# Local transformer: one head pair a step, or two pairs a step with keys kept in place

## The chip, the cores and the metric

The kernel runs on one core of one Trainium2 chip, in one launch. The metric is the device time in microseconds (us) of the whole launch; lower is better. Engines are named as in the profile: PE (matrix multiplies; PEld its weight loads), DVE, ACT and POOL (element-wise work; ACT also has the exponential and the GELU), SP (issues the DMAs).

## The reference, cut to what matters

The program is a stack of four blocks over `x` of 16 sequences, 256 tokens, 128 channels, in float32. Block 1 (a linear attention with an MLP), block 3 (multi-query attention) and block 4 (an MLP) are the same before and after the change. Block 2 is a local transformer of six layers, and all of the change lies there:

```python
for i in range(6):
    x = attn_layer(shift_tokens(x), Wqkv[i], q_scale[i], k_scale[i], Wo[i]) + x
    x = ffn_layer(shift_tokens(x), ...) + x
# attn_layer: 16 heads of 64 channels
q = l2norm(q) * qs;  k = l2norm(k) * ksc
q = q * cos * scale + rotate_half(q) * sin * scale
k = k * cos / scale + rotate_half(k) * sin / scale
# local_attention: windows of 32 queries see 64 keys (their own window and the one before)
sim = einsum(bq, bk2) * 8; sim = where(mask, -max, sim)
out = einsum(softmax(sim), bv2);  return out @ Wo
```

## The kernel before, in words

The 16 sequences are eight units of two (512 tokens). A unit's state `z` (128 channels on the partitions) stays in SBUF through the six layers, with 32 columns of zeros ahead of each sequence. The work of block 2 goes in steps, one for each layer, unit and pair of heads: 6 x 8 x 8 = 384 steps. The main loop is the `while` at the end of the stage (from L986); step `n` starts pair `n` and carries on older pairs, so that some ten pairs are in flight:

- `project` (pair n): two multiplies make q and k of the pair in two PSUM banks (L645). From each bank DVE makes the sine part `sent` (L646) and the cosine part (L650; `q` or `k`), and ACT the squares (`sq`, L652). Four DMAs (L656, L657) swap the halves of `sent` between partitions into `got`.
- `rotate` (pair n-1): POOL adds `got` to q and to k (L662).
- Every fourth step `norms_sum` (L670) sums the squares of four pairs on PE with the selector `sel`; `norms_inverse` makes inverse square roots (transposes L688, small POOL operations L706 to L714); one step later `norms_rows` (L722, L724) sends the keys' ones to DRAM.
- `widened` (pair n-6): two DMAs (L733) bring a key factor to all rows, `kn`.
- `scaled` (pair n-7): POOL multiplies k by kn into one of two padded buffers, `kf` (L744). The seven buffers of the unpadded k come free only with this operation.
- `masked`, `softmax` (pair n-8): a bf16 multiply writes the mask into two PSUM banks (`sim`, L770; one bank for each head, half of it used), and 32 small multiplies add the scores (L785; each in two passes, so 64 instructions), for which PE works as eight tiles of 64x32. Then the maxima (L797), `nb` (L801, maximum times factor) and eight exponentials with their sums (L803, ACT).
- `divided` (L815, L817): reciprocal on DVE, product on POOL. `flipped` (pair n-9): four transposes (L826) and a copy into `prT` (L832 or L834).
- `attended`, a generator for each unit that moves one place a step: `windows` transposes the state (L755); the weighted sums `mm<-prT,xw` (L864, 64x128 tiles) are made for 64 tokens a step; eight multiplies a step (L847, `y`) merge heads. The values and the output weight are multiplied ahead, in `merge_vo`. After it `ffn` (L902 to L955), also one place a step.

PE is thus used whole (128x128) for projections, merging, transposes and the feed-forward part, and in tiles for L864, L670 and L785. PSUM has four banks for everything called `mm`, three for `sim`, one for `y`.

The order on each engine is made when the program is built, by a planner: the source order is a priority, and an instruction whose inputs, by the planner's own cost tables, are not ready is passed by a later one. On the chip each engine then follows the fixed order and waits where it must. In the trace this is seen where twelve passes of L785 stand ahead of L864, although the source has all of L864 first.

Of the kernel before, what the change touches and what calls it, by code (L numbers as in the profile page):

```python
# [10 lines left out]
F32 = mybir.dt.float32  # L11
# [8 lines left out]
NU = B // 2  # L20
# [24 lines left out]
def adaln_kernel(  # L45
# [504 lines left out]
    with ExitStack() as es:  # L550
# [25 lines left out]
        kfs = [persistent(f"kf{j}", (128, 2, PAD + L)) for j in range(2)]  # L576
# [58 lines left out]
        def project(i, u, wqk):  # L635
# [3 lines left out]
            rows, squares = [], []  # L639
            sent, got = atile("sent", (128, 2, 512)), atile("got", (128, 2, 512))  # L640
            for j, name in enumerate(("q", "k")):
# [7 lines left out]
                r = atile(name, (128, 512), 8 - j)  # L649
                nc.vector.scalar_tensor_tensor(two(r), two(pp), scale, tab[0], ALU.mult, ALU.mult)  # L650
                sq = work("sq")
                nc.scalar.activation(sq, pp, AF.Square)  # L652
                rows.append(r)
# [4 lines left out]
            return rows, squares, got  # L658

        def rotate(rows, got):  # L660
            for j in range(2):
                nc.gpsimd.tensor_tensor(rows[j], rows[j], got[:, j, :], ALU.add)  # L662
# [19 lines left out]
        def norms_inverse(n2):  # L682
# [34 lines left out]
            return rk, rq.rearrange("p (a b) t -> p a b t", b=2)  # L717
# [11 lines left out]
        def widened(j, home):  # L729

            kn = atile("kn", (128, 512))
            for par in range(2):
                nc.sync.dma_start(  # L733
                    kn[64 * par : 64 * par + 64, :],
                    home[2 * j + par : 2 * j + par + 1]
                    .rearrange("e t p -> e (t p)")
                    .to_broadcast([64, 512]),
                )
            return kn

        def scaled(m, k, kn):

            kf = kfs[m % 2]
            nc.gpsimd.tensor_tensor(kf[:, :, PAD:], two(k), two(kn), ALU.mult)  # L744
            return kf
# [20 lines left out]
        def masked():  # L766
            sims = []
            for par in range(2):
                sim = pss.tile([128, 512], F32, tag="sim", name="sim")[:, 0:256]
                nc.tensor.matmul(  # L770
                    sim, ident16, maskb, start=True, stop=False, skip_group_check=True
                )
                sims.append(sim)
            return sims

        def softmax(sims, q, kf, rn):

            q = two(q)
            for st in range(4):
                s = st // 2  # L780
                for c in range(4):
                    t0 = (st % 2) * 128 + 32 * c
                    for par in range(2):
                        r = slice(64 * par, 64 * par + 64)
                        nc.tensor.matmul(  # L785
                            sims[par][32 * c : 32 * c + 32, st * 64 : (st + 1) * 64],
                            q[r, s, t0 : t0 + 32],
                            kf[r, s, t0 : t0 + 64],
                            start=False,
# [3 lines left out]
            pr = atile("pr", (128, 4, 2, 64))  # L793
            ssum = small("ssum", (128, 4, 2))
            for par in range(2):
                mx = small("mx", (128, 4))
                nc.vector.tensor_reduce(  # L797
                    mx, sims[par].rearrange("p (b k) -> p b k", b=4), AX.X, ALU.max
                )
                nb = small("nb", (128, 4))  # L800
                nc.vector.scalar_tensor_tensor(nb, mx, -1.0, rn[:, par, :], ALU.mult, ALU.mult)  # L801
                for st in range(4):
                    nc.scalar.activation(  # L803
                        pr[:, st, par, :],
                        sims[par][:, st * 64 : (st + 1) * 64],
                        AF.Exp,
                        bias=nb[:, st : st + 1],
                        scale=rn[:, par, st : st + 1],
                        accum_out=ssum[:, st, par : par + 1],
                    )  # L810
            return pr, ssum

        def divided(pr, ssum):
            rsum = small("rsum", (128, 8))
            nc.vector.reciprocal(rsum, ssum.rearrange("p t h -> p (t h)"))  # L815
            prf = pr.rearrange("p t h k -> p (t h) k")
            nc.gpsimd.tensor_tensor(  # L817
                prf, prf, rsum.unsqueeze(2).to_broadcast([128, 8, 64]), ALU.mult
            )
            return pr  # L820

        def flipped(p, pr, prT):

            pt = bank()
            for st in range(4):
                nc.tensor.transpose(  # L826
                    pt[:, st * 128 : (st + 1) * 128],
                    pr[:, st].rearrange("p h k -> p (h k)"),
                    ident,
                )  # L830
            if p % 2:
                nc.vector.tensor_copy(prT[:, p, :], pt)  # L832
            else:
                nc.scalar.copy(prT[:, p, :], pt)  # L834

        def attended(u, prT, vo):


            xw = windows(u, 0)
            yield  # L840
            py = psy.tile([128, 512], F32, tag="y", name="y")
            zxs = {}
            for k in range(10):
                if k >= 2:
# [11 lines left out]
                if k < 8:  # L856
                    if k % 2 == 0:
                        zxs[k // 2] = atile("zx", (128, 2, NP, 128))
# [555 lines left out]
```

## Time and profile before

| what | us |
|---|---|
| median of three runs (4742.04 to 4749.64) | 4749.21 |
| the profiled execution | 4745.02 |
| its span, first to last instruction | 4743.2 |
| first and last start of the projections L645 | 407.5 and 3987.2 |
| PE, DVE, ACT, POOL busy | 4280.3, 2887.7, 2922.1, 2621.8 |
| L645, L847, L864, L785 busy on PE | 772.7, 753.9, 533.1, 360.7 |
| L803 busy on ACT (exponentials, and reading their sums) | 1195.6 and 639.5 |
| L662 (q and k), L744, L817 busy on POOL | 488.4 and 489.2, 490.9, 400.7 |

The span runs from the first to the last instruction of one profiled execution; 1.8 us of that execution lie around it. PE's busy time counts pipelined multiplies as overlapping stretches, so 90% is not PE at its peak. Idle time is given with the instruction that ended it.

### The profile page before, as it was taken

What the parts mean: (1) busy time and instruction counts of PE and PEld (TensorE: products, weight loads), DVE (VectorE), ACT (ScalarE), POOL (GpSimd) and SP (SyncE); (2) the same over time, 40 slices, a digit from 0 to 9 for tenths busy, and PEclk for the clock granted to TensorE, in tenths of its full rate; (3) what the DMA queues carried; (4) which work ended last, traced back from release to release, by engine and by line L of the source; (5) the groups of instructions that cost most, each with busy time, mean ns of one, the idle gap of its engine ahead of it and who ended that gap; (6) DMA issues with size and microseconds to landing.
All of it is one profiled execution on the core that took longest, in us unless ns stands there. A gap on an engine that the chain in (4) does not pass through costs nothing.

```text
span 4743.2 us, 121371 instructions
## 1 busy us (share of the span) xinstructions
PE 4280.3 (90%) x46105; PEld 2711.0 (57%) x46105; DVE 2887.7 (61%) x6755; ACT 2922.1 (62%) x9846; POOL 2621.8 (55%) x3296
## 2 busy tenths in 40 slices
PE   6677689999999999999999999999999999799998
PEld 4443356666666666666666666666666666455454
DVE  3434456666676666766666666666666666455554
ACT  2332456666666666666666666666666666277776
POOL 3323556666666666666666666656666665044342
PEclk7678789999999999999999999999999999899999
DMA  1023234433433334444344343333433333200000
GB/s 29 5 34 93 75 77 104 98 100 93 102 98 100 98 98 100 100 97 98 95 101 100 96 102 95 98 98 96 102 95 98 94 96 82 64 1 6 5 3 7
DMA packets 193567, 371.25 MB, mean 78 GB/s; under 512 B 42537, under 2 KB 83416, under 8 KB 192984
## 3 DMA queue, kind: packets, MB, share of 16 engines
q1 hardware_dynamic: 192984, 363.50, 31.2%
q8 instruction: 364, 5.96, 0.5%
q14 instruction: 219, 1.79, 0.1%
HBM read 127.92 MB, written 8.91 MB: 29 GB/s over the span
## 4 chain that ended last, share of the span: by engine, by line
PE 37%; POOL 16%; ACT 15%; issue 13%; DVE 10%; DMA 5%; SPq 2%; POOLq 0%; DVEq 0%; ACTq 0%
ACT pr L803 7%; PE mm L864 5%; PE y L847 4%; PE mm L645 3%; PE sim L785 3%; POOL kf L744 3%; POOL q L662 3%; DMA got<-sent 3%; POOL k L662 2%; PE mm L955 2%; PE mm L670 2%; DVE mx L797 2%; PE mm L945 2%; POOL pr L817 2%; DVE sent L646 2%
## 5 line engine op out<-in xcount | busy, mean ns | idle before, releaser
L803 ACT ACTIVATE pr<-sim,nb,rq 128x64 f32<-128x64 f32 x3072 | 1195.6, 409 | 521.5 <-DVE nb L801 470.5
L645 PE MATMUL mm<-z,wqk 128*128 128x512 f32 x1536 | 772.7, 626 | 4.0 <-DMA wqk<-in_L_ffn_Wqkv_dram 3.1
L847 PEld LDWEIGHTS y<-zx,wvo 128*128 128x128 f32 x6144 | 728.6, 192 | 74.4 <-issue 72.4
L847 PE MATMUL y<-zx,wvo 128*128 128x128 f32 x6144 | 753.9, 276 | 1.2 <-ACT zx L879 1.2
L817 POOL TENSOR_TENSOR pr<-pr,rsum 128x512 f32<-128x512 f32 x384 | 400.7, 1043 | 500.3 <-DVE rsum L815 468.4
L803 ACT ACTIVATION_READ_ACCUMULATOR pr<-sim,nb,rq 128x1 f32 x3072 | 639.5, 208 | 0.0
L662 POOL TENSOR_TENSOR q<-q,got 128x512 f32<-128x512 f32 x384 | 488.4, 1272 | 248.1 <-DMA got<-sent 219.0
L646 DVE SCALAR_TENSOR_TENSOR sent<-mm,vec,rope 128x512 f32<-128x512 f32 x768 | 569.2, 742 | 45.5 <-PE mm L645 36.6
L864 PE MATMUL mm<-prT,xw 64*128 64x256 f32 x3072 | 533.1, 406 | 66.6 <-ACT sq L652 65.4
L652 ACT ACTIVATE sq<-mm 128x512 f32<-128x512 f32 x768 | 437.3, 620 | 237.2 <-DVE k L650 205.8
L744 POOL TENSOR_TENSOR kf<-k,kn 128x512 f32<-128x512 f32 x384 | 490.9, 1279 | 123.5 <-PE sim L785 55.8
L877 DVE COPY zx<-mm 128x512 f32<-128x512 f32 x384 | 262.8, 684 | 433.1 <-PE mm L864 429.7
L662 POOL TENSOR_TENSOR k<-k,got 128x512 f32<-128x512 f32 x384 | 489.2, 1274 | 0.0
L864 PEld LDWEIGHTS mm<-prT,xw 64*128 64x128 f32 x3072 | 324.4, 186 | 249.5 <-issue 103.8
L650 DVE SCALAR_TENSOR_TENSOR k<-mm,vec,rope 128x512 f32<-128x512 f32 x384 | 285.0, 742 | 261.7 <-POOL kf L744 259.4
L797 DVE TENSOR_REDUCE mx<-sim 128x4 f32<-128x256 f32 x768 | 289.8, 419 | 232.9 <-PE sim L785 224.9
L785 PEld LDWEIGHTS sim<-kf,q 64*32 64x32 f32 x24576 | 280.3, 107 | 263.5 <-issue 177.5
L879 ACT COPY zx<-mm 128x512 f32<-128x512 f32 x384 | 227.6, 593 | 300.2 <-PE mm L864 300.0
L785 PE MATMUL sim<-kf,q 64*32 64x64 f32 x24576 | 360.7, 227 | 46.8 <-POOL kf L744 46.5
L645 PEld LDWEIGHTS mm<-z,wqk 128*128 128x128 f32 x1536 | 267.8, 195 | 224.9 <-issue 153.2
L1174 POOL TENSOR_TENSOR pr<-pr,rsum 128x256 f32<-128x256 f32 (+1 forms) x256 | 206.4, 828 | 318.8 <-DVE rsum L1172 294.4
L706 POOL TENSOR_TENSOR na<-nx,ny 128x64 f32<-128x64 f32 x288 | 92.4, 321 | 405.2 <-DVE ny L699 390.1
(237 smaller groups left out, 6973.7 us busy)
## 6 DMA issues: line engine op xcount, KB each, us to landing
got<-sent SPq DMA_DIRECT2D x1536, 128.0 KB
kn<-rkh SPq DMA_DIRECT2D x768, 128.0 KB
xw<-xw SPq DMA_DIRECT2D x96, 256.0 KB
wqk<-in_L_ffn_Wqkv_dram SPq DMA_DIRECT2D x48, 128.0 KB
bhome<-brow SPq DMA_DIRECT2D x1, 3072.0 KB
wv<-in_L_ffn_Wqkv_dram SPq DMA_DIRECT2D x12, 256.0 KB
wo<-in_L_ffn_Wo_dram SPq DMA_DIRECT2D x12, 256.0 KB
xt<-in_x_dram SPq DMA_DIRECT2D x8, 256.0 KB
```

What stands on the lines that cost most here:

```text
L645: nc.tensor.matmul(pp, wqk[:, j, :], xs, start=True, stop=True)
L646: nc.vector.scalar_tensor_tensor(two(sent[:, j, :]), two(pp), scale, tab[1], ALU.mult, ALU.mult)
L650: nc.vector.scalar_tensor_tensor(two(r), two(pp), scale, tab[0], ALU.mult, ALU.mult)
L652: nc.scalar.activation(sq, pp, AF.Square)
L662: nc.gpsimd.tensor_tensor(rows[j], rows[j], got[:, j, :], ALU.add)
L744: nc.gpsimd.tensor_tensor(kf[:, :, PAD:], two(k), two(kn), ALU.mult)
L785: nc.tensor.matmul(sims[par][32 * c : 32 * c + 32, st * 64 : (st + 1) * 64], q[r, s, t0 : t0 + 32], kf[r, s, t0 : t0 + 64], start=False, s ...
L797: nc.vector.tensor_reduce(mx, sims[par].rearrange("p (b k) -> p b k", b=4), AX.X, ALU.max)
L803: nc.scalar.activation(pr[:, st, par, :], sims[par][:, st * 64 : (st + 1) * 64], AF.Exp, bias=nb[:, st : st + 1], scale=rn[:, par, st : st ...
L817: nc.gpsimd.tensor_tensor(prf, prf, rsum.unsqueeze(2).to_broadcast([128, 8, 64]), ALU.mult)
L847: nc.tensor.matmul(py[:, st * 128 : (st + 1) * 128], vo[:, h, :], zxs[st][:, h % 2, h // 2, :], start=(h == 0), stop=(h == 2 * NP - 1), sk ...
L864: nc.tensor.matmul(pz[par][:, j * 256 : (j + 1) * 256], xw[r, (2 * k + j) % 8, :], prT[r, :, 64 * k + 32 * j : 64 * k + 32 * j + 32], star ...
```

## The change

Steps of two pairs: 192 steps in place of 384 (`QS = NP // 2`). The parts of a step are put in a new order, written out by hand: first the whole-array work (merging, transposes of probabilities, norms' rows, feed-forward, windows, mask), then the tiled work in one stretch (weighted sums, every second step the sums of squares, the scores), then norms' transposes, feed-forward and the two projections. The softmax is split in functions; the exponentials of head 0 of both pairs are placed ahead of the first projection, those of head 1 between the projections, the division after them. Maxima, `nb`, mask and division handle two pairs in one instruction. `attended` is replaced by `weighted` and `merging`, called from the loop. The feed-forward generator is moved twice a step, and its GELUs (L941) join the piece of the gate multiplies before them (L934) (`go_on(behind)`).

Keys are written by `project` into eight padded buffers `ks`, rotated there and multiplied by `kn` there; the copies `kf` and their two buffers go. `pr` has one buffer of 1024 columns in place of two of 512. The selector and the index `e` are permuted to match. The diff, cut to its core:

```diff
-        kfs = [persistent(f"kf{j}", (128, 2, PAD + L)) for j in range(2)]
+        ks = [persistent(f"k{j}", (128, 2, PAD + L)) for j in range(8)]
...
+            q = two(atile("q", (128, 512), 8))
+            k = ks[m % 8][:, :, PAD:]
...
-                r = atile(name, (128, 512), 8 - j)
-                nc.vector.scalar_tensor_tensor(two(r), two(pp), scale, tab[0], ALU.mult, ALU.mult)
+                nc.vector.scalar_tensor_tensor(r, two(pp), scale, tab[0], ALU.mult, ALU.mult)
...
-            kf = kfs[m % 2]
-            nc.gpsimd.tensor_tensor(kf[:, :, PAD:], two(k), two(kn), ALU.mult)
+            k = ks[m % 8][:, :, PAD:]
+            nc.gpsimd.tensor_tensor(k, k, two(kn), ALU.mult)
...
+            if 0 <= n - 4 < N:
+                for x in range(2):
+                    scaled(2 * (n - 4) + x, kns.pop(2 * (n - 4) + x))
             if 0 <= n - 1 < N:
-                rotate(rows[n - 1], got.pop(n - 1))
+                for x in range(2):
+                    m = 2 * (n - 1) + x
+                    rotate(m, qs[m], got.pop(m))
...
+                merging(j, range(NP), zxs[w, j], vos[w // NU], pys[w])
+            if 0 <= n - 5 < N:
...
+                flipped(p, prs.pop(n - 5), prTs[i, u])
+            if at_w:
+                merging(j, range(NP, 2 * NP), zxs.pop((w, j)), vos[w // NU], pys[w])
...
+            if n % 2 and 3 <= n <= N + 1:
+                home = norms_rows(rk)
+            go_on(behind)
+            go_on(merges)
...
+                    xws[v, s] = windows(v % NU, s)
+            sims = masked() if 0 <= n - 4 < N else None
...
+                zxs[v, r] = weighted(r, xws[v, r // 2], prTs[v // NU, v % NU])
+            if n % 2 == 0 and 2 <= n <= N:
+                n2 = norms_sum([squares.pop(m) for m in range(2 * n - 4, 2 * n)])
+            if sims:
+                m = 2 * (n - 4)
+                rn = inverses[m // 4][:, m % 4 // 2]
+                scores(sims, m, [qs.pop(m), qs.pop(m + 1)])
+                pr = atile("pr", (128, 2, 4, 2, 64), 1)
+                ssum = small("ssum", (128, 2, 4, 2))
+                nbs = [maxima(sims[par], rn[:, par]) for par in range(2)]
+                exponentials(0, sims[0], nbs[0], rn[:, 0], pr, ssum)
+
+            if n % 2 == 0 and 2 <= n <= N:
+                rk, inverses[n // 2 - 1] = norms_inverse(n2)
+            if at_w and j == QS - 1:
+                behind.append(ffn(w % NU, w // NU, *wff))
+            go_on(behind)
             if n < N:
...
+                qs[m], squares[m], got[m] = project(i, u, m, wqk[p])
+            if sims:
+                exponentials(1, sims[1], nbs[1], rn[:, 1], pr, ssum)
+            if n < N:
+                m = 2 * n + 1
+                qs[m], squares[m], got[m] = project(i, u, m, wqk[p + 1])
+            if sims:
+                divided(pr, ssum)
+                prs[n - 4] = pr
+            if 0 <= n - 3 < N:
+                for m in (2 * (n - 3), 2 * (n - 3) + 1):
+                    kns[m] = widened(m, home)
```

New functions that it calls:

```python
def maxima(sim, rn):
    mx = small("mx", (128, 8))
    nc.vector.tensor_reduce(mx, sim.rearrange("p (b k) -> p b k", b=8), AX.X, ALU.max)
    nb = small("nb", (128, 8))
    nc.vector.scalar_tensor_tensor(nb, mx, -1.0, rn, ALU.mult, ALU.mult)
    return nb

def exponentials(par, sim, nb, rn, pr, ssum):
    for x in range(2):
        for st in range(4):
            b = 4 * x + st
            nc.scalar.activation(pr[:, x, st, par, :], sim[:, b * 64 : (b + 1) * 64], AF.Exp,
                bias=nb[:, b : b + 1], scale=rn[:, b : b + 1],
                accum_out=ssum[:, x, st, par : par + 1])

def weighted(j, xw, prT):
    zx = atile("zx", (128, 2, NP, 128))
    for k in (2 * j, 2 * j + 1):
        pz = [bank(), bank()]
        ...  # the four multiplies of L864 and the two copies of L877, L879, as before
    return zx

def merging(j, heads, zx, vo, py):
    for h in heads:
        nc.tensor.matmul(py[:, j * 128 : (j + 1) * 128], vo[:, h, :], zx[:, h % 2, h // 2, :],
            start=(h == 0), stop=(h == 2 * NP - 1), skip_group_check=True)
```

## The prediction

> **What bounds the kernel now.** The page first: its span, and PE's row.
>
> ```profile
> span 4743.2 us, 121371 instructions
> PE 4280.3 (90%) x46105; PEld 2711.0 (57%) x46105; DVE 2887.7 (61%) x6755; ACT 2922.1 (62%) x9846; POOL 2621.8 (55%) x3296
> ```
>
> PE is the engine with least room. The source view of the projections runs from 407.5 to 3987.2 us, so the 384 pairs take 3580 us: 9.32 us a pair, 18.65 for two pairs, 74.6 for a unit of eight. Only these 3580 us are touched; the other 1165 of the profiled 4745 stay. The table of stretches for them:
>
> ```profile
> 407.00:3987.00 3580.00, 3307.13 (x41019) 2156.73 (x41020) 2337.93 (x4760) 2297.85 (x8020) 2240.20 (x2842) 0.98 0.39 97
> ```
>
> PE 92%, the others 63 to 65%: no other engine becomes the bound by its sum, since none gains much work. What PE loses is read from its timeline (start, duration with overlap, instruction):
>
> ```profile
> 2213.64 1.95 PE L847 MATMUL y<-zx,wvo 128*128 128x128 f32 x16
> 2215.42 0.38 PE L770 MATMUL sim<-maskb,ident 128*128 128x256 bf16 x2
> 2215.73 1.14 PE L864 MATMUL mm<-prT,xw 64*128 64x256 f32 x8
> 2216.80 0.86 PE L785 MATMUL sim<-kf,q 64*32 64x64 f32 x64
> 2217.59 1.98 PE L645 MATMUL mm<-z,wqk 128*128 128x512 f32 x4
> ```
>
> Sixteen passes of L847 take 1.78 us from start to start, 0.111 each; so L770's two end at 2215.64 and the tiles start 0.09 late. Four pass times of 256 columns, side by side on two row tiles, would be 0.86 (the six passes of 512 of L955 just before take 2.58, 0.43 each), but L785 starts after 1.07: 0.21 lost. The last score pass runs out before L645: some 0.14 of its 0.216. Entering, changing and leaving tiles costs about 0.44 a pair.
>
> The waits of PE over the same stretch, largest first (us, times, longest):
>
> ```profile
> PE mm L670 <- ACT sq L652: 71.7, 46, 2.7
> PE mm L864 <- ACT sq L652: 65.4, 86, 1.1
> PE sim L785 <- POOL kf L744: 46.5, 15, 5.7
> PE sim L770 <- ACT pr L803: 30.6, 48, 1.2
> PE mm L945 <- ACT sq L652: 23.8, 29, 1.1
> ```
>
> Most end with a square. Behind L670's stands this, in the timeline around 2241 us:
>
> ```profile
> 2239.90 1.26 POOL L744 TENSOR_TENSOR kf<-k,kn 128x512 f32<-128x512 f32 x1
> 2241.20 0.75 DVE L650 SCALAR_TENSOR_TENSOR k<-mm,vec,rope 128x512 f32<-128x512 f32 x1 [4.05 <-POOL kf L744]
> ...
> 2241.99 0.60 ACT L652 ACTIVATE sq<-mm 128x512 f32<-128x512 f32 x1 [2.40 <-DVE k L650]
> ...
> 2242.64 3.62 PE L670 MATMUL mm<-sq,sel 128*32 128x512 f32 x16 [2.36 <-ACT sq L652]
> ```
>
> A new k needs one of seven buffers, free only after L744; DVE stands 4.05 us, the square behind it, then PE. L650 waits so 116 times, 259.4 us in all. All the waits of PE there make about 260 us, 5.4 a unit.
>
> **What the skill says.** The Trainium skill, TensorEngine Tiling (Array Packing), Key Properties: changing the tiling mode drains TensorE. The 0.09, 0.21 and 0.14 agree. TensorE: Matmul & The Clock Gate, Part 1: a PE idle for a window of about 3.4 us falls to half clock. Here 2.36 us of idleness sufficed: L670's 16 passes took 3.62 where they take 1.92 elsewhere. SBUF — State Buffer, Who interferes with whom: a DVE instruction with two SBUF inputs blocks behind a GpSimd one that reads SBUF. `nb` (L801) is one: median 152 ns, mean 334, longest 1267, about one POOL product.
>
> **The change part by part, for two pairs.**
>
> *Work.* Multiplies, transposes, exponentials, squares, copies and DMAs are as many as before. Two L797 of 419 ns become one of 512 columns for each head, at about 0.68 (L877, 512 columns from PSUM, takes 684), four `nb` become two, two reciprocals one: DVE saves under 1 us, hidden under PE. L770 has half as many instructions of double width: nothing. Key products into rows of 2x256: L744 wrote such rows at 1279 ns, against 1274 for flat L662: nothing. Six more buffers to clear: a few us once on POOL, before its first rotation; if not covered, that.
>
> *Tiles.* One stretch in place of two saves 0.44, 192 x 0.44 = 84 us if the order holds. If one whole-array instruction falls inside, 0.09 + 0.21 come back.
>
> *Keys.* The wait for L744 goes: k's buffer is free when the scores of four steps ago are done, and these stand before the projection on PE. What is late next is the square itself: those of the second projection come behind the second set of exponentials on ACT, and the sums of squares want them some 6 us of PE work later. Of the 166 us of PE's waits on squares (five lines, three of them above) I take 105 as gone, 2.2 a unit; bounds 0 and 166, plus some 20 for the slow clock.
>
> *Queues.* Rotations have a step of 18.65 us instead of 9.32 for their transfers. `got` has two buffers, both used in one step now, but their refill comes a step later, behind the rotation. SP issues eight `got` and four `kn` DMAs a step at about 0.6 us: 7.2 of 18.65. `kn` is issued at the end of a step and wanted before the scores of the next, with `scaled` first on POOL. Nothing new is late.
>
> *Softmax.* This is where the change adds a wait. From the last score to the transposes of its probabilities:
>
> - DVE: two maxima, 2 x 0.68 = 1.36, and `nb`, 0.3 to 0.7: 1.9 with ACT's start;
> - ACT: eight exponentials 0.382 apart (2219.17 to 2219.57 and on, from ACT's timeline): 3.06; two squares that stand between, 1.11; eight more, 3.06;
> - DVE reciprocal and its handing on, 0.4; POOL, 1024 columns at twice L817's 1.04: 2.1.
>
> Sum 11.6 us. Before it was about 5.5 with a step of 9.3 and the projection to cover it; `flipped` stood after the next projection. Now it stands after 8 heads of merging. In source order PE has for cover: norms' transposes 0.22, four projections' passes 2 x 1.72 = 3.44, half the feed-forward (538 us busy over six lines, 11.2 a unit, 2.8 a step) 1.4, merging 1.78: 6.8. PE would stand 4.8 us. Then transposes 0.88, merging 1.78, feed-forward 1.4, windows 0.44, mask 0.43, L864 2.0, half of L670 0.92, scores 1.44: 9.3. Step 11.6 + 9.3 = 20.9, or 2.25 more than 18.65: 192 x 2.25 = +430 us.
>
> But the planner does not hold source order. Three lines of PE's timeline:
>
> ```profile
> 2222.05 0.33 PE L785 MATMUL sim<-kf,q 64*32 64x64 f32 x12
> 2222.92 1.62 PE L864 MATMUL mm<-prT,xw 64*128 64x256 f32 x8 [0.54 <-ACT sq L652]
> 2224.46 0.76 PE L785 MATMUL sim<-kf,q 64*32 64x64 f32 x52
> ```
>
> L864 is ahead of L785 in the source; the planner, expecting it late, passed it, and on the chip it was later still by 0.54. So I expect it to pass `flipped` with the second merging, feed-forward, windows and mask, 1.78 + 1.4 + 0.44 + 0.43 = 4.05: cover 10.85 against 11.6. The transposes land at the door of the tiled stretch, PE waiting 0.7, or just inside it at 0.3 for two more changes. But they stand where the planner's tables say ready, with no slack; what the chip does later is all wait. Bounds: 0, and some 1.7 (nb blocked twice by POOL adds 2 x 1.1 to the chain, less what PE's own lateness gives). I take 0.4 a step.
>
> *Sum for a unit*: tiles -0.9 (half of 4 x 0.44), keys -2.2, softmax +1.6 (4 x 0.4): -1.5. Times 48 = -72, on 4745: 4673; the profiled run is 4 below the median of 4749, so 4677.
>
> **The rivals.**
>
> 1. *The softmax's chain reaches PE.* Same mechanism with a larger wait. It decides at (0.9 + 2.2) x 48 / 192 = 0.78 us a step at the transposes; above it the change loses. For: zero slack, chain doubled, POOL's products across `nb`. Against: the 9.5 us for which PE waited at L826 in the whole stage before. At 1.5 us: 192 x (1.5 - 0.78) = +138, 4887. With source order in full, 4749 + 430 = 5180. Chance 0.30 for the first, 0.12 for the second.
> 2. *PE's waits nearly go*: tiles whole (-84), squares (-166, and -20 of slow clock), transposes 0.3 (+58): -212, 4537. For: twice the time for every transfer and norm. Against: ACT still has the gates (three copies of 0.58, three GELUs of 0.72, two table loads of 1.28: 6.5 us in one piece, once a unit) ahead of copies that free `mm` banks. Chance 0.12.
> 3. *The change does not do what it says*: the planner strews whole-array work through the stretch (no gain from tiles) and the squares' wait goes over to the banks that they hold: within 0.2%, 4749. Chance 0.06.
>
> The forecast has 0.40.
>
> **How the numbers follow.** Faster 0.40 + 0.12, same 0.06, slower 0.42; 0.2%, 9 us, is about what three runs can tell. Likeliest: 4677, its own range 4600 to 4735 (keys from 0 to all, wait from 0 to 0.75). The range for 8 in 10: down to 4510 for the second rival with a little more, up to 4920 for waits to 1.7 us; left out are source order (0.12) and the tails.
>
> **What would show it.** Right: L785 and L864 with no L826 between, starts of L864 0.3 later half as often; no wait of L650 on POOL; L670's wait on squares under 25 us; L826's wait on POOL's `pr` under 80 us (192 x 0.4). Wrong: L826 (or whatever stands there) waiting 200 us or more; a PE clock below 0.98 in the stage; a step over 18.65 us. If `mm` banks rule, L864 or L902 will wait on ACT's copies and squares.

## The result, and the profile after

| | us |
|---|---|
| before, median of 4 runs (4742.04 to 4750.96) | 4749.43 |
| after, median of 4 runs (4961.98 to 4982.88) | 4973.42 |
| after / before, 95% interval | 1.0474 [1.0449, 1.0498] |
| the profiled execution of after, and its span | 4973.54, 4971.8 |
| first and last start of the projections (L647) after | 408.6 and 4229.5 |

The change makes the kernel 224 us slower. The whole loss lies in block 2: its projections start over 3821 us where they took 3580. A step of two pairs takes 19.9 us against 18.65.

The page of after, its span and PE's row:

```profile
span 4971.8 us, 118780 instructions
PE 4346.0 (87%) x45721; PEld 2814.7 (57%) x45721; DVE 2782.6 (56%) x5795; ACT 2929.3 (59%) x9846; POOL 2586.0 (52%) x3110
```

PE has 384 instructions fewer and is busy 66 us longer; the rest of the span, in which it is not busy, grew from 462.9 to 625.8 us. A busy time that grows with less work to do can be a sign of the clock. The table of stretches, the same columns as before (PE, PEld, DVE, ACT, POOL busy, then the granted clock as a share of full speed, the DMA share and GB/s):

```profile
407.00:4229.00 3822.00, 3379.57 (x40687) 2263.61 (x40688) 2239.14 (x3827) 2308.70 (x8036) 2203.19 (x2658) 0.92 0.36 91
```

The clock fell from 0.98 to 0.92. The two longest waits of PE over this stretch (us, times, longest):

```profile
PE mm L834 <- POOL pr L825: 331.3, 143, 5.1
PE sim L769 <- ACT pr L812: 50.1, 59, 6.9
```

The waits on squares, which made three of the five lines shown of before, are gone; one wait that was 9.5 us there is now 331: the transposes of the probabilities (`flipped`, L834) for the division on POOL (L825). DVE's wait of 259.4 us for a free k buffer is no longer among DVE's waits at all. PE's timeline shows one such wait, and what follows it:

```profile
2228.20 1.48 PE L791 MATMUL sim<-k,q 64*32 64x64 f32 x128
...
2230.97 3.60 PE L647 MATMUL mm<-z,wqk 128*128 128x512 f32 x8
2234.40 3.73 PE L873 MATMUL y<-zx,wvo 128*128 128x128 f32 x32
2237.97 0.59 PE L769 MATMUL sim<-maskb,ident 128*128 128x512 bf16 x2
2238.50 0.90 PE L791 MATMUL sim<-k,q 64*32 64x64 f32 x68
2242.25 1.51 PE L834 MATMUL mm<-ident,pr 128*128 128x128 f32 x8 [2.86 <-POOL pr L825]
...
2243.77 1.71 PE L906 MATMUL mm<-mean,fs 128*128 128x1 f32 x8
2245.41 0.42 PE L791 MATMUL sim<-k,q 64*32 64x64 f32 x4
2245.76 1.91 PE L753 MATMUL mm<-ident,z 128*64 128x128 f32 x8
```

Three things are to be seen. PE goes on from the last score of a step at 2229.62 and starts its transposes at 2242.25, 12.63 us later; PE has work for 9.77 of them. The step is typical: counted in the trace, the transposes wait in 147 of the 192 steps, and over these the mean is 12.30 us, of which 9.99 are covered. Work of the next step has been put ahead of the transposes: both halves of the merging (L873), the mask (L769), here half of the scores (L791). The feed-forward piece (L906) and the windows (L753), which do not need the division either, stand behind. And the tiled stretch that the change wanted in one piece is broken: scores (L791) stand on both sides of the transposes.

The chain itself, from scores to divided probabilities, is on the other engines' timelines. DVE's maxima start at 2229.71 (two in 1.29 us), `nb` follows at 2231.03 and 2231.58 (0.50 and 1.17 us, the second beside a POOL product). ACT runs the first eight exponentials from 2231.64, three squares from 2234.71 and the other eight from 2236.67 to 2239.7; DVE's reciprocal starts at 2239.90. The last step of it, on POOL:

```profile
2240.30 1.90 POOL L825 TENSOR_TENSOR pr<-pr,rsum 128x1024 f32<-128x1024 f32 x1 [2.09 <-DVE rsum L823]
```

POOL stood idle for 2.09 us before the division: it was the chain that was late, not POOL. Counted in the trace, it stood so before the division in 144 of the 147 steps that wait.

### The profile page after: what moved, and what is told of

It is laid out like the page before. It is cut to its first block, busy times and chain, and to the rows that moved or that the text cites. A ratio compares the mean times of both kernels' runs of the same rounds, so it can differ in the third digit from the quotient of the medians.

```text
span 4971.8 us, 118780 instructions
## 1 busy us (share of the span) xinstructions
PE 4346.0 (87%) x45721; PEld 2814.7 (57%) x45721; DVE 2782.6 (56%) x5795; ACT 2929.3 (59%) x9846; POOL 2586.0 (52%) x3110
## 4 chain that ended last, share of the span: by engine, by line
PE 42%; ACT 21%; POOL 9%; issue 9%; DVE 7%; DMA 3%; SPq 2%; POOLq 0%; DVEq 0%; ACTq 0%
ACT pr L812 13%; POOL pr L825 6%; PE mm L834 5%; PE mm L647 4%; PE mm L852 4%; PE y L873 4%; PE mm L670 4%; DMA kn<-rkh 3%; PE mm L951 3%; PE mm L930 2%; PE mm L941 2%; ACT sq L653 2%; PE sim L791 2%; PE mm L753 2%; DVE sent L648 2%
## 5 line engine op out<-in xcount | busy, mean ns | idle before, releaser
L873 PEld LDWEIGHTS y<-zx,wvo 128*128 128x128 f32 x6144 | 721.5, 192 | 99.4 <-issue 92.1
L825 POOL TENSOR_TENSOR pr<-pr,rsum 128x1024 f32<-128x1024 f32 x192 | 365.3, 1903 | 764.8 <-DVE rsum L823 708.3
L873 PE MATMUL y<-zx,wvo 128*128 128x128 f32 x6144 | 728.6, 275 | 0.6 <-ACT zx L867 0.5
L647 PE MATMUL mm<-z,wqk 128*128 128x512 f32 x1536 | 699.0, 597 | 3.3 <-DMA wqk<-in_L_ffn_Wqkv_dram 2.5
L743 POOL TENSOR_TENSOR k<-k,kn 128x512 f32<-128x512 f32 x384 | 488.4, 1280 | 208.7 <-DMA kn<-rkh 207.6
L834 PE MATMUL mm<-ident,pr 128*128 128x128 f32 x1536 | 249.5, 315 | 338.8 <-POOL pr L825 338.8
L852 PE MATMUL mm<-prT,xw 64*128 64x256 f32 x3072 | 464.1, 432 | 13.3 <-ACT fg L932 8.7
L647 PEld LDWEIGHTS mm<-z,wqk 128*128 128x128 f32 x1536 | 283.8, 191 | 326.5 <-issue 217.6
L834 PEld LDWEIGHTS mm<-ident,pr 128*128 128x128 f32 x1536 | 197.5, 159 | 412.2 <-POOL pr L825 412.2
L791 PEld LDWEIGHTS sim<-k,q 64*32 64x32 f32 x24576 | 283.0, 106 | 185.8 <-issue 114.1
L840 DVE COPY prT<-mm 128x512 f32<-128x512 f32 x192 | 132.3, 689 | 419.9 <-PE mm L834 419.9
L803 DVE TENSOR_REDUCE mx<-sim 128x8 f32<-128x512 f32 x384 | 244.7, 679 | 211.8 <-PE sim L791 210.8
L791 PE MATMUL sim<-k,q 64*32 64x64 f32 x24576 | 344.1, 227 | 16.3 <-POOL k L743 14.1
```

The lines of the kernel that those rows point to most:

```text
L647: nc.tensor.matmul(pp, wqk[:, j, :], xs, start=True, stop=True)
L743: nc.gpsimd.tensor_tensor(k, k, two(kn), ALU.mult)
L791: nc.tensor.matmul(sims[par][32 * c : 32 * c + 32, c0 : c0 + 64], q[r, s, t0 : t0 + 32], k[r, s, t0 : t0 + 64], start=False, stop=True, sk ...
L825: nc.gpsimd.tensor_tensor(prf, prf, rsum.unsqueeze(2).to_broadcast([128, 16, 64]), ALU.mult)
L834: nc.tensor.transpose(pt[:, st * 128 : (st + 1) * 128], pr[:, x, st].rearrange("p h k -> p (h k)"), ident,)
L852: nc.tensor.matmul(pz[par][:, w * 256 : (w + 1) * 256], xw[r, (2 * k + w) % 8, :], prT[r, :, 64 * k + 32 * w : 64 * k + 32 * w + 32], star ...
```

## The experiments

Each run has its own runs of the kernel before on the same chip (medians 4742 to 4749); ratios are to those. Four questions were put: is the key part good by itself, is the wait at the transposes the cause of the loss, what puts it there, and is there a version that keeps the good parts.

### The keys alone, and a price for a break in the tiled stretch

`keys` is the kernel before with its keys rotated and normalised in place:

```diff
-        kfs = [persistent(f"kf{j}", (128, 2, PAD + L)) for j in range(2)]
+        ks = [persistent(f"k{j}", (128, 2, PAD + L)) for j in range(8)]
...
-                r = atile(name, (128, 512), 8 - j)
+                r = ks[m % 8][:, :, PAD:] if j else two(atile(name, (128, 512), 8))
...
-            kf = kfs[m % 2]
-            nc.gpsimd.tensor_tensor(kf[:, :, PAD:], two(k), two(kn), ALU.mult)
+            nc.gpsimd.tensor_tensor(k, k, two(kn), ALU.mult)
```

> The kernel before with one part of the change alone: keys written, rotated and multiplied in place in eight padded buffers, steps of one pair as before. If the wait of the new k on POOL was worth what the forecast took: L650 no longer waits for POOL, PE's waits on squares fall from 166 us to under 60, and the time by 60 to 130 us, to 4620 to 4690. If the wait only hid another (the transfer of got, the rotation): 4735 to 4760.

Measured: 4589.18 us, ratio 0.9671 [0.9654, 0.9687], so -156 us, 26 more than the forecast's upper end. Two of the waits of PE from 407 to 4229 us, which takes in the whole of block 2:

```profile
PE sim L769 <- ACT pr L801: 46.8, 56, 4.3
...
PE mm L862 <- ACT sq L652: 20.9, 44, 1.1
```

Of the waits on squares one line of 20.9 us is left near the top; in all they fell by 135 us, from 166 to 32. Other waits took some 40 back, the largest at the transposes for POOL's product, from 9.5 to 41.9. The gain splits by the page into time in which PE is not busy, 462.9 to 360.4 (-102.5), and busy time, 4280.3 to 4227.0 (-53.3), with the same instructions. The clock can account for about half of the busy part: from 1000 to 3500 us the granted clock is 1.00 before and here, and over the projections' stretch it is 0.98 and 0.99. The trace's clock records, which know full and half speed only, have half speed there for 142 us before and for 86 here; half of the difference, 28 us, is the most that this can be worth. The rest stands mainly where the squares' waits stood: the weighted sums are busy 511.2 us for 533.1, the sums of squares 191.9 for 206.8. Why is not shown.

`maskmid` is `keys` with the mask product moved from ahead of the weighted sums to between them and the scores:

```diff
-            sims = masked() if 0 <= n - 8 < N else None
             for g in again:
                 if next(g, running) is running:
                     running.remove(g)
+            sims = masked() if 0 <= n - 8 < N else None
```

> The kernel of keys (4589), with its one whole-array mask product put ahead of the scores, between the tiled weighted sums and the tiled scores, instead of ahead of the weighted sums: two more changes between whole-array and tiled work in each of the 384 pair steps. Theory A (a change costs 0.09 to 0.15 us, as the trace of before shows between these rows): +35 to +58 us, 4624 to 4647. Rival 1 (the change costs nothing that PE does not wait for anyway): 4589 +/- 8. Rival 2 (both drains are paid in full, 0.3 us a step): 4704.

Measured: 4623.25, ratio 0.975 [0.9736, 0.9765], 34 us above `keys`, just below the lower end of what theory A gave. But the planner did not keep the mask there in all of the 384 steps: counted in the trace, PE goes over from whole-array to tiled work (L862, L670, L783) 727 times, where it does so 502 times in `keys`. So 225 breaks cost 34 us, 0.15 each. PE's busy time rose by more, 64 us (4227.0 to 4291.0) or 0.28 a break; time in which it is not busy fell by 25, since the mask, now later, waits less for ACT (46.8 to 21.6). Breaking the stretch is a real cost, and it does not explain the loss: the changed kernel goes over to tiled work 391 times, less often than `keys`, if not the 192 times that were planned.

### Is it the wait at the transposes?

From `keys` to the changed kernel is +384 us. By the pages' spans, 4587.4 to 4971.8, it is 265.4 us of time in which PE is not busy and 119.0 of busy time. The following runs test whether both are the wait at L834.

`nodiv` leaves out the product of the division (L825); its probabilities stay unnormalised:

```diff
-            prf = pr.rearrange("p x t h k -> p (x t h) k")
-            nc.gpsimd.tensor_tensor(
-                prf, prf, rsum.unsqueeze(2).to_broadcast([128, 16, 64]), ALU.mult
-            )
```

> The changed kernel without the product of the division on POOL (L825, 192 products of 1.90 us), so the outputs are built on probabilities that are not normalised; the reciprocal stays. The chain is 1.9 us shorter, and POOL has 365 us less to do. Theory A (as for asplit): the wait at the transposes falls from 339 us by nearly 147 x 1.9 = 279, to under 100, and the time by that and up to half again, to 4560 to 4700. Rival (another wait of the same length stands behind it): above 4850.

Measured: 4544.09, ratio 0.9568 [0.9547, 0.9589], 429 us below the changed kernel and a little below theory A's range. The first line of PE's waits (the transposes are L830 here):

```profile
PE mm L830 <- ACT pr L812: 45.7, 45, 1.6
```

339 us of waits at the transposes become 46, and the time goes with them. Time in which PE is not busy falls by 329 us, busy time by 97. It is not only that the chain is 1.9 us shorter. The product over all 1024 columns tied the eight transposes of a step together; without it each needs only its own two exponentials, and the planner strews them one at a time between merging, mask and scores:

```profile
2223.29 0.33 PE L830 MATMUL mm<-ident,pr 128*128 128x128 f32 x1
2223.55 0.33 PE L791 MATMUL sim<-k,q 64*32 64x64 f32 x12
2223.81 0.33 PE L830 MATMUL mm<-ident,pr 128*128 128x128 f32 x1
```

So `nodiv` shows what the wait was worth, and not what 1.9 us of chain are worth. It also shows again that broken tiled work is not what cost the time: PE goes over to it 716 times here. The table of stretches for 1000 to 3500 us shows the clock, first the changed kernel, then `nodiv`:

```profile
1000.00:3500.00 2500.00, 2240.87 (x27018) 1510.19 (x27018) 1481.39 (x2529) 1530.99 (x5318) 1445.74 (x1739) 0.93 0.36 91
```

```profile
1000.00:3500.00 2500.00, 2443.03 (x30348) 1611.12 (x30346) 1649.40 (x2847) 1711.59 (x5992) 1367.41 (x1820) 1.00 0.41 102
```

The clock is enough to explain the busy part. In the stretch of the projections the trace records half speed for 612 us in the changed kernel, 90 in `nodiv` and 86 in `keys`; with PE busy in them these cost at most 284, 33 and 32 us. The differences, 251 and 252, are more than the 97 and 119 by which busy time differs, since the order pulls the other way: the changed kernel's projections are busy 699.0 us for 764.9 in `keys` and its weighted sums 464.1 for 511.2, and the strewn transposes of `nodiv` 416.6 for 249.5. How clock is lost can be seen in the changed kernel's timeline:

```profile
2204.97 1.76 PE L834 MATMUL mm<-ident,pr 128*128 128x128 f32 x8 [1.96 <-POOL pr L825]
...
2206.74 3.69 PE L941 MATMUL mm<-fx,w 128*128 128x512 f32 x6
```

After 1.96 us of idleness eight transposes take 1.76 us, where they take 1.04 at 2221 us, and the six passes of L941 take 3.69, where six passes of 512 columns (L951) take 2.84 at 2213 us. The clock records have 3.41 us at half speed there, from 2205.2.

There is a further reservation: without its product POOL also has 365 us less to do. `asplit` keeps the product and shortens the chain in another way, by doing the softmax pair by pair: exponentials of both heads of the first pair, its division, then the second pair, with tiles of their own.

```diff
-                exponentials(1, sims[1], nbs[1], rn[:, 1], pr, ssum)
+                divided(pr[0], ssum[0])
+                exponentials(1, sims, nbs, rn, pr[1], ssum[1])
...
-                divided(pr, ssum)
+                divided(pr[1], ssum[1])
```

> The changed kernel with the softmax pair by pair (as in split), the transposes left where the change has them. Theory A (the time over keys, 385 us, is the wait at the transposes and the clock lost by it, so time follows the wait): the first pair's transposes find their data and the second's come about 1 us earlier in each of the 147 waiting steps, so the wait falls from 339 us by 147 or more, to 100 to 190, and the time by as much and up to half again for the clock, to 4750 to 4830. Rival (PE then waits for something else that is as late: bank, keys, mask): the wait falls but the time stays above 4900.

Measured: 4863.41, ratio 1.0245 [1.0221, 1.0268], 110 us below the changed kernel. Both theories missed. The wait did not shrink, it went to pieces:

```profile
PE mm L834 <- POOL pr L825: 355.3, 239, 8.3
```

239 waits of 1.5 us in place of 147 of 2.3, since now each of the two groups of transposes can wait. The planner also used up what the shorter chain gave: counted in the trace, 168 of these waits stand between the two halves of the merging, the place of the source, where in the changed kernel one of the 147 does. Time not busy fell by only 33 us; busy time fell by 75, and the clock from 1000 to 3500 us rose from 0.93 to 0.97. Here the same sum of waits in shorter pieces went with less loss of clock: half speed followed 66 of the 239 waits, none of them under 1 us, against 113 of the 147.

Two smaller suspects were tried one at a time. `pr2` gives `pr` two buffers (and, to make room, the pool of squares 9 in place of 11); `a_kn` issues the DMAs that spread the keys' norms (`widened`, L734) at the head of a step, right after `norms_rows`, ahead of the rotation's eight copies.

```diff
-                pr = atile("pr", (128, 2, 4, 2, 64), 1)
+                pr = atile("pr", (128, 2, 4, 2, 64), 2)
```

> The changed kernel with two buffers of probabilities instead of one and nothing moved (pool of squares 9 instead of 11). Theory A: the chain and the place of the transposes are the same, so the wait stays at 300 to 340 us and the time at 4940 to 5000. Theory C (the single buffer is to blame: the next exponentials cannot start before the transposes): wait under 150 us, 4700 to 4850.

> The changed kernel with one move: the DMAs that spread the keys' norms are issued at the head of the step, ahead of the rotation's copies. Theory A (POOL waits 208 us for these DMAs with the softmax's division queued behind, so part of the wait at the flipped transposes is theirs): that wait falls from 339 us to 150 to 280 and the time from 4973 to 4780 to 4920. Rival (POOL's wait on them ends before the exponentials do, and the division waits for its sums either way): 4960 to 4985.

Measured: `pr2` 4957.55, ratio 1.0439 [1.0411, 1.0466], with 323.0 us of waits at L834; `a_kn` 4940.09, ratio 1.0414 [1.0396, 1.0431], with 330.1. The single buffer does not hold the transposes up. `a_kn` lies between the ranges of its two theories, and it does not test what it was meant to: POOL's waits on these DMAs are 207.5 us in it and 207.6 in the changed kernel. That the late norms do not hold up the division is seen from POOL's idle time before it in the changed kernel, of which 708 us of 765 end with the reciprocal.

### What puts the wait there?

The planner may pass an instruction that it expects late, and it did pass the transposes with merging, mask and scores, but with nothing that needs one of the four shared PSUM banks called `mm`. `bank()` is the call that takes one of them. In the built program their order is a rule nearly without exception: of 3658 tiles called `mm`, only 8 are first written out of the order of the source, in the kernel before as in the changed one. Merging writes the bank `y`, mask and scores write `sim`. `bank` gives the transposes a bank of their own, taken from `mm`; `mm3` is its control, which only takes the bank away.

```diff
-        pss = psum(es, 4, 3)
+        pss = psum(es, 3, 3)
...
-                pt = bank()
+                pt = pss.tile([128, 512], F32, tag="fl", name="fl", bufs=1)
```

> The changed kernel with the flipped transposes in a PSUM bank of their own, taken from the four that all other whole-array work shares. Theory A (those banks are handed out in the order of the source, so that feed-forward, windows, norm rows and weighted sums can't be put ahead of the waiting transposes): with its own bank the planner can put them ahead, the wait at the transposes on POOL's pr falls from 339 us to under 170, and the time to 4650 to 4850 in spite of the bank less. Rival (the planner takes this order by its own estimate of when the division is done): the wait stays above 300 us and the time at 4950 to 5050.

> The control of bank: the changed kernel with three shared PSUM banks instead of four, the transposes still in them. Theory A (the order of the banks holds the transposes, their number does not): the wait at the transposes stays at 300 to 400 us, and the time is 4970 to 5080. Rival (it is the number of banks that shapes the order): the wait falls as in bank.

Measured: `mm3` 5098.74, ratio 1.0748 [1.0732, 1.0764], with a wait of 274.7 us at L834; `bank` 5064.95, ratio 1.0676 [1.066, 1.0692]. `bank`'s first line of PE's waits, and its timeline around one group of transposes (`fl`):

```profile
PE fl L834 <- POOL pr L825: 97.9, 114, 5.5
```

```profile
2217.59 1.13 PE L930 MATMUL mm<-fx,w 128*128 128x512 f32 x2
2219.43 0.66 PE L834 MATMUL fl<-ident,pr 128*128 128x128 f32 x4 [0.72 <-POOL pr L825]
2219.93 1.02 PE L930 MATMUL mm<-fx,w 128*85 128x512 f32 x2
2220.88 1.13 PE L852 MATMUL mm<-prT,xw 64*128 64x256 f32 x4
```

With a bank of their own, feed-forward and weighted sums stand ahead of the transposes, and the wait falls by two thirds. So the order of the banks is what kept `mm` work behind them. The time did not follow: it is 34 us below the control and 92 above the changed kernel. A bank less costs 125 us by itself (`mm3` lies 19 us above its forecast, with a wait 25 below). Beside that control other waits grew in `bank`, at the mask for ACT from 50.6 to 95.3 us and at the scores for POOL's k from 18.1 to 54.5, so that time not busy fell by only 45 us, and busy time rose by 16. The work is also cut into scraps: L930 and the transposes, each one piece elsewhere, stand here in turns. Part of that is the test's own: both groups of transposes share one bank, and 37 times the second waits for the copy of the first. What the scraps cost is not shown. Theory A was right on the wait and wrong on the time.

`move` goes the other way: the four shared banks stay, and the source puts the transposes later, behind the mask, right ahead of the weighted sums.

```diff
-            if 0 <= n - 5 < N:
-                i, u, p = place(n - 5)
-                ...
-                flipped(p, prs.pop(n - 5), prTs[i, u])
             if at_w:
...
             sims = masked() if 0 <= n - 4 < N else None
+            if 0 <= n - 5 < N:
+                i, u, p = place(n - 5)
+                ...
+                flipped(p, prs.pop(n - 5), prTs[i, u])
```

> The changed kernel with flipped moved down in the same step, from between the two mergings to behind the mask, just ahead of the weighted sums; buffers as changed. Theory A: norms' rows, feed-forward and windows, some 1.9 us of PE work a step, may now stand ahead of the transposes, since their banks are asked for first; the wait falls by up to 192 x 1.9 = 365 us, less where there was no such work: to 60 to 200 us, the time to 4700 to 4850. Theory B: no gain, 4940 to 5000.

Measured: 4663.45, ratio 0.9828 [0.9812, 0.9844]: 310 us below the changed kernel, from a change of place alone. That is 37 us better than theory A's range. The wait is 176.7 us, and the clock of the middle 2500 us is 0.99. By the pages, time not busy falls by 171 us and busy time by 134. Of the tests of the wait this is the cleanest: the chain, the buffers and the work are those of the changed kernel. With `move` the second half of the merging, feed-forward and windows come before the transposes in the source, as the prediction had expected the planner to arrange.

### Versions that keep the good parts

`split` is `move` with the pair by pair softmax of `asplit`; `split_kn` also issues the norms' DMAs early.

> The flipped transposes stand behind the mask product, as in move (4663), and the softmax goes pair by pair: the first pair's 512 columns are exponentiated and divided first, on POOL in two operations of half the size, with tiles of their own. Theory A (the chain behind the last score still reaches PE, 177 us of PE's wait on POOL's pr in move): half of the transposes find their data ready and the other half's chain is about 1 us shorter (half of a 1.9 us division), so that row falls from 177 to about 50 us and the time to 4540 to 4600. Rival (what move leaves over the 4589 of keys is the whole-array work in one stretch, not the softmax): the row falls but the time stays at 4640 to 4670.

> split, with the DMAs that spread the keys' norms issued at the head of the step instead of at its end, ahead of the rotation's copies on their queue. Theory A (POOL's k <- kn wait, 208 us in the changed kernel, stands in POOL's order ahead of the division): POOL's waits on kn fall below 60 us, the division comes sooner, and the time is 20 to 50 us under split's. Rival (POOL has slack there): within 10 us of split.

Measured: `split` 4534.35, ratio 0.9566 [0.955, 0.9582], with 93.2 us left at the transposes; `split_kn` 4507.39, ratio 0.9505 [0.949, 0.9519]. `split` ends 6 us below theory A's range, though its wait is nearer 100 than 50. `split_kn` gains the 20 to 50 us that theory A gave, but not in its way: POOL's waits on `kn` fell from 228 to 201 us only, not below 60, so where the gain comes from stays open.

`lag` leaves the transposes where the change has them but takes the probabilities of a step earlier, so that the chain has a whole step more; windows, weighted sums and merging follow a step later, and `pr` has two buffers, the pool of squares 9. In `lag` the first unit of each layer after the first takes the feed-forward weights of the layer before; the work is the same. `lag_kn` loads these weights a step earlier, so that each unit has its own, and issues the norms' DMAs at the head of the step.

```diff
-            if 0 <= n - 5 < N:
-                i, u, p = place(n - 5)
+            if 0 <= n - 6 < N:
+                i, u, p = place(n - 6)
...
+            if 0 <= n - 3 < N:
+                for m in (2 * (n - 3), 2 * (n - 3) + 1):
+                    kns[m] = widened(m, home)
             go_on(behind)
```

> The changed kernel with the transposes of the probabilities, and all that follows them, one step later (flipped for pair step n-6, windows, weighted sums and merging one step on), which takes two buffers of probabilities; to make room, the pool of squares has 9 buffers instead of 11. Theory A (PE stands at the transposes for the softmax's chain of 12.6 us, since nothing that needs an mm bank may pass them): the wait of the transposes on POOL falls from 339 us to under 30, the granted clock of the block's 3800 us rises from 0.92 to 0.97 or more, and the time falls by the 330 us and some 50 to 120 us of slow clock: 4520 to 4600. Theory B (PE's time went to the tiled stretch being broken up, and to the order as such; the idle time only happens to be shown at the transposes): 4850 or more, the wait turning up elsewhere.

> lag (4924: flipped transposes a step later, which took the wait at them away and put 238 us of waits at the scores on POOL's scaled keys in its place), with the spread of the keys' norms issued at the head of the step. Theory A (the keys come late because their DMAs are queued behind the rotation's copies): the scores' wait falls from 238 to under 60 us, the time to 4600 to 4740. Rival (POOL stands in order at the division, which waits for the exponentials' sums, with the scaled keys queued behind it): the scores' wait stays above 150 us and the time above 4850.

Measured: `lag` 4923.78, ratio 1.0378 [1.0361, 1.0394]; `lag_kn` 4464.01, ratio 0.9413 [0.9398, 0.9427], the fastest of all. `lag` was forecast at 4520 to 4600 and missed by over 300. `lag_kn` was forecast at 4600 to 4740 and came out 136 below. In `lag` the wait at the transposes for POOL is gone, and this took its place:

```profile
PE sim L791 <- POOL k L743: 238.5, 97, 7.8
```

The same line of `lag_kn`:

```profile
PE sim L791 <- POOL k L743: 11.7, 9, 2.3
```

Here the early DMAs, with the earlier load of the weights, are worth 460 us; in `a_kn`, with the older wait still in place, they were worth 33. A wait that is not the last to end shows its price only when the one behind which it hides is gone. What the early DMAs do has two parts that the runs do not tell apart: the transfers are issued ahead of eight `got` copies on their queue, and the planner puts the scaling products elsewhere on POOL. POOL's timeline of `lag` ahead of a score that waited 4.41 us:

```profile
2241.12 1.26 POOL L662 TENSOR_TENSOR k<-k,got 128x512 f32<-128x512 f32 x1
2242.34 1.26 POOL L743 TENSOR_TENSOR k<-k,kn 128x512 f32<-128x512 f32 x1
```

The product that the scores wait for stands right behind a rotation (from 2239.90), and this behind ten small norm operations (from 2235.94). `lag_kn_split` adds the pair by pair softmax to `lag_kn`:

> lag_kn (4464) with the softmax pair by pair as in split. Theory A (with the transposes a step later the softmax's chain is off PE's path, so a shorter one is worth nothing): 4464 +/- 15. Rival (POOL, which stands at the division for 469 us in lag_kn, still sets the pace through the keys it scales behind it): 4400 to 4445.

Measured: 4469.10, ratio 0.9418 [0.9404, 0.9432], level with `lag_kn` (4464.01), as theory A said: with the transposes no longer waiting for POOL, a shorter chain was worth nothing here.

In `lag_kn` the two-pair step comes near to what it was made for: counted in the trace, PE goes over to tiled work 250 times. In the step shown, PE's timeline has transposes, merging, mask, all weighted sums and all scores in that order, with no idle time among them:

```profile
2212.02 1.04 PE L834 MATMUL mm<-ident,pr 128*128 128x128 f32 x8
2212.89 1.95 PE L873 MATMUL y<-zx,wvo 128*128 128x128 f32 x16
...
2214.79 0.59 PE L769 MATMUL sim<-maskb,ident 128*128 128x512 bf16 x2
2215.32 2.00 PE L852 MATMUL mm<-prT,xw 64*128 64x256 f32 x16
2217.24 1.59 PE L791 MATMUL sim<-k,q 64*32 64x64 f32 x128
```

Against `keys` PE is busy 115.5 us less (4227.0 to 4111.5), with the clock from 1000 to 3500 us at 1.00 in both.

## Why the prediction was wrong

The forecast was 4677 us; the first rival, at 4887, had the mechanism that came true; the measured 4973 is above both, and above 4920, the end of the range.

**The failed step** is in the softmax part: "So I expect it to pass `flipped` with the second merging, feed-forward, windows and mask". The planner passed the transposes with merging and mask, and with half or more of the next scores, which the prediction had not named; feed-forward (1.4 in the sum) and windows (0.44) stayed behind, since they need an `mm` bank, and these go in the order of the source. The built program shows the order, and `bank` shows that it held the work back. So the cover was not the 10.85 us of the sum but 9.99, the mean of the 147 steps that wait. That is about half of what was missed in a step that waits; the other half is the chain. The prediction's last sentence, "If `mm` banks rule, L864 or L902 will wait on ACT's copies and squares", named the resource and looked for its effect in the wrong place.

**The chain** was put at 11.6 us and measured 12.30 in the mean of those steps, 12.63 in the one shown. There most terms were sound: maxima 1.29 for 1.36, exponentials 3.07 and 3.05 for 3.06 each, division 1.90 for 2.1. Between the two sets of exponentials stand three squares, 1.96, instead of two at 1.11, one of them the feed-forward's. The prediction's own difference, 11.6 less 10.85, is a wait of 0.75 us. The missing cover adds 0.86 and the longer chain 0.70, which makes the 2.31 us of a mean wait.

**The softmax term** of 0.4 us a step measured 339 / 192 = 1.76 as a wait, just over the upper bound of 1.7, and more as time. The 0.4 was already below the 0.75 of the prediction's own sum, although it said in the same place that the planner leaves no slack; `asplit` bears that remark out. Rival 1's formula with 1.76 gives 4749 + 192 x (1.76 - 0.78) = 4937. It leaves out the clock: the half-speed time after an idle PE was named for the squares and not for the transposes. `nodiv` puts the wait with its clock at some 429 us, 2.2 us a step, with the reservations above. A wait of over 0.78 us a step made the change lose, as rival 1 said; it was given 0.30.

**The keys term**, 2.2 us a unit, 105 us, measured 156 in `keys`: the mechanism was right. That idle time fell by 102.5, so near to 105, is in part luck: 135 us of waits on squares went and some 40 came back as other waits. The 53.3 us of busy time were not in the term; the clock is at most 28 of them.

**The tiles term**, 0.9 us a unit, taken as half of 84 us, can't be read from the changed kernel, where the slow clock lies over it. PE goes over to tiled work 391 times there, for 501 before and 192 planned, so a part of it may have come. With 250, in `lag_kn`, PE is busy 115.5 us less than in `keys`, though its order differs in more than that. `maskmid` priced a break at 0.15 us in time and 0.28 in busy time, against 0.3 in the prediction's working.

**The queues.** "Nothing new is late" was wrong in a way that the changed kernel hides. With the transposes' wait taken away (`lag`), the keys' scaling is late by 238 us of waits at the scores.

**The clock.** The Trainium skill, TensorE: Matmul & The Clock Gate, Part 1, gives an idle window of about 3.4 us for the fall of the clock. The prediction had already seen 2.36 suffice; after the change 1.96 did, ahead of L834 and L941. Half speed followed 113 of the 147 waits there. A wait of two microseconds can thus cost nearly as much again (3.41 us at half speed is 1.7 us of lost work), and that belonged into the sum.

## What to carry to other kernels

When a change lengthens a chain that one engine waits for, list what really may pass the waiting instruction: where buffers of one name are handed out in source order, as here, work that needs one can't, however ready it is. Price a wait on PE with the clock that it costs after it: here busy time grew by 119 us on 265 of idleness, although the new order saved some. And when a wait is moved away, look for what it was hiding before trusting the result: nearly the same edit was worth 33 us with the wait in place and 460 without it.

## What the runs showed of the hardware

Idle stretches of 2 us already cost the clock: after 1.96 us of idleness eight transposes took 1.76 us instead of 1.04, and the six passes after them 3.69 instead of 2.84. In the six traces where they were looked up (before, after, `keys`, `nodiv`, `asplit`, `move`) the half-speed periods of block 2 last 3.41 us or a whole multiple of it. At the transposes they followed 113 of 147 waits in the changed kernel (mean 2.3 us), 66 of 239 in `asplit` (mean 1.5) and 32 of 147 in `move` (mean 1.2), and in the last two none of the 155 waits under 1 us. A whole-array product put between two tiled stretches cost 0.15 us of time and 0.28 of PE's busy time each, over 225 of them, in `maskmid`.
